# An audio tower on one core: odd DCT coefficients from 128 rotated samples, expert tiles in single PSUM banks

## The chip, the cores and the metric

The kernel runs on one core of a Trainium2 chip. The time is device microseconds of one execution; the median of three runs of the kernel before is 1459.71 us (1459.28 to 1461.03). Everything is fp32. Five engines work side by side, each through its own queue in order: TensorE (PE in the profile; its weight loads are PEld), VectorE (DVE), ScalarE (ACT), GpSimd (POOL) and SyncE (SP, which here only issues DMAs). They wait for each other through semaphores.

## The reference

64 clips of 80,000 samples are cut into 157 frames of 512 samples (the last is padded with zeros). Each frame goes through an orthonormal DCT of 512 points, and the result through one layer of attention and one of experts:

```python
h = einsum('bfh,kh->bfk', frames, DCT)          # 64 x 157 x 512
h = h + attention(layernorm(h))                  # phasor memory, causal sums, sigmoid gate, Wo
h = h + experts(layernorm(h))                    # each clip: mean over frames picks one of 16 experts
```

In the attention, keys and queries are 32 phases each; a causal sum over the frames of phase products weighs the values x Wv, a gate sigmoid(x Wg) mixes two such reads, and the result goes through Wo. In the experts, the mean of a clip's rows is routed by a softmax over 16 logits; the clip's rows are multiplied with the chosen 512 x 512 matrix and scaled by the gate.

## The kernel before

The clips go in 16 groups of four. A group has five tiles of 128 rows: the first 128 frames of each of its four clips (tiles 0 to 3), and tile 4 with the four tails of 29 frames, at 32 rows each.

**Order.** The schedule is written out by hand: instructions stand in each engine's queue in the order in which the program issues them. Group g's iteration consists of `project_and_values(g)` (projections, values; beside it routing of group g-1), `gate(g)`, `experts_and_embedding(g)` (L885: the experts of group g-1, the DCT of group g+1) and `attention(g)`. Group 0 has `first_values` and `first_gate` in place of the first three, and group 15 has no embedding, so `experts_and_embedding` runs for g = 1 to 14.

**The DCT.** `load_frame` (L85) brings a tile's samples, transposed and partly reversed by the host, as four blocks of 128 samples by 128 frames. `fold_once` (L91) makes sums `even` on VectorE (L96) and differences on GpSimd (L97, in place, blocks 0 and 1). `fold_twice` (L100) folds the sums once more on VectorE into blocks 2 and 3. `embed` (L189) then needs two matmuls with 128 columns for the even coefficients (4j and 4j+2, L201), and, for the odd ones, two matmuls with 256 columns that are summed in PSUM (L203): 256 differences against 256 odd coefficients. An fp32 matmul stands in the profile as two passes, so that L201 and L203 have four passes each for a tile. All land in one bank `h`, each coefficient in its place by a stride of four.

**The norm.** `embed_ln` (L206) takes `statistics` (L150: VectorE's bn_stats L153 and bn_aggr L155, then three small GpSimd operations L157, L158 and L160 for the reciprocal deviation `rstd` and `shift`), one more GpSimd operation for `rstd1`, and two ScalarE activations of `h`: `x`, the normed tile (L213), and `r`, the residual with the norm added (L220). `turn` (L228) transposes x with four TensorE transposes (L166) and `place` (L169) copies the result to SBUF on ScalarE (L172, L174).

**The stage of experts and embedding** issues steps in this order: E0 D0 D1 E1 T0 D2 E2 T1 D3 E3 T2 D4 E4 T3. E is `expert(g-1, m)` (L757: eight passes of 512 columns at L185, or 32 for the tails at L766, then VectorE's eviction with gate and bias L774 and the store); D is `embed`, `embed_ln` and `load_frame`; T is `turn`. After D1, D2 and D3 and T0 it also issues `fold_once` and `fold_twice` for tiles 3 and 4, `add_bias` (L755, VectorE) and `add_bv` (L348, GpSimd, 2.36 us each). `attention` begins with `read_tails(0)`, then T4, then `read_tails(2)`. The folds of tiles 0 to 2 stand in `project_and_values` and `gate`.

**PSUM.** `psum()` hands out three tiles of two banks in turn, `bank()` two single banks in turn. The embeddings, experts, products and reads use `psum()`; transposes, scores and routing use `bank()`. A tile is handed out again when its last reader is through.

Of the kernel before, what the change touches and what calls it, by code (L numbers as in the profile page):

```python
# [14 lines left out]
F32 = mybir.dt.float32  # L15
I32 = mybir.dt.int32
AF = mybir.ActivationFunctionType
ALU = mybir.AluOpType
AX = mybir.AxisListType

B, L, D = 64, 157, 512
T_IN = 80000
P = 128
# [3 lines left out]
NG = B // GB  # L27
# [3 lines left out]
NM = GB + 1  # L31
# [10 lines left out]

@with_exitstack
def audio_tower(ctx: ExitStack, tc: tile.TileContext, a, out):

# [22 lines left out]
    def load(name, shape, src=None):  # L70
        t = const.tile(shape, F32, name=name, tag=name)
        nc.sync.dma_start(out=t, in_=a[name] if src is None else src)
        return t

    def psum():

        return ps_mm.tile([P, 2, 512], F32, tag="mm", name="mm")
# [22 lines left out]
    def fold_twice(g, m):  # L100

        if g < NG:
            ft, even = S[g]["frame", m], S[g].pop(("even", m))
            nc.vector.tensor_tensor(ft[:, 2, :], even[:, 0, :], even[:, 1, :], ALU.add)
            nc.vector.tensor_tensor(ft[:, 3, :], even[:, 0, :], even[:, 1, :], ALU.subtract)


    load_frame(0, 0)
    dct_e = load("dct_e", [P, 2, P])
    dct_o = load("dct_o", [P, 2, 2 * P])  # L110
    load_frame(0, 1)
    load_frame(0, 2)
    wv = load("wv", [P, C, D])
# [36 lines left out]
    def statistics(h):  # L150

        st = small.tile([P, 6], F32, tag="st", name="st")
        nc.vector.bn_stats(st, h)  # L153
        mv = small.tile([P, 2], F32, tag="mv", name="mv")
        nc.vector.bn_aggr(mv, st)  # L155
        rstd = small.tile([P, 1], F32, tag="rstd", name="rstd")
        nc.gpsimd.tensor_scalar(rstd, mv[:, 1:2], EPS, None, ALU.add)  # L157
        nc.gpsimd.tensor_tensor(rstd, rstd, power, ALU.pow)  # L158
        shift = small.tile([P, 1], F32, tag="shift", name="shift")
        nc.gpsimd.tensor_scalar(shift, mv[:, 0:1], rstd, -1.0, ALU.mult, ALU.mult)  # L160
        return rstd, shift
# [27 lines left out]
    def embed(g, m):  # L189

        s = S[g]
        if m == 0:
            s["xT"] = p1.tile([P, C, GB, LP], F32, tag="xT", name="xT", bufs=2)
            s["xT_t"] = p1.tile([P, C, P], F32, tag="xT_t", name="xT_t")
            s["res"] = []
            s["res2"] = []
        h = psum()[:, 0, :]
        ft = s.pop(("frame", m))
        by_r = h.rearrange("p (j r) -> p r j", r=4)
        for i in range(2):  # L200
            nc.tensor.matmul(by_r[:, 2 * i, :], ft[:, 2 + i, :], dct_e[:, i, :], start=True, stop=True)  # L201
        for i in range(2):
            nc.tensor.matmul(by_r[:, 1::2, :], ft[:, i, :], dct_o[:, i, :], start=(i == 0), stop=(i == 1))  # L203
        s["h", m] = h

    def embed_ln(g, m):  # L206
        s = S[g]
        h = s.pop(("h", m))
        rstd, shift = statistics(h)
        rstd1 = small.tile([P, 1], F32, tag="rstd1", name="rstd1")  # L210
        nc.gpsimd.tensor_scalar(rstd1, rstd, 1.0, None, ALU.add)
        x = p2.tile([P, D], F32, tag="x", name="x")
        nc.scalar.activation(x, h, AF.Identity, bias=shift, scale=rstd)  # L213
        if m == GB:
            r = p1.tile([P, D], F32, tag="res_t", name="res_t", bufs=2)
        else:
            if m % 2 == 0:
                s["res2"].append(p1.tile([P, 2, D], F32, tag="res", name="res", bufs=4))
            r = s["res2"][-1][:, m % 2, :]
        nc.scalar.activation(r, h, AF.Identity, bias=shift, scale=rstd1)  # L220
        s["res"].append(r)
        s["x", m] = x
# [214 lines left out]
    fold_once(0, 1)  # L437
    fold_twice(0, 1)
    embed(0, 1)
    embed_ln(0, 0)  # L440
    warm(6)
    fold_once(0, 2)
    turn(0, 0)
    embed_ln(0, 1)
    fold_twice(0, 2)
    embed(0, 2)
    fold_once(0, 3)
    value(0, 0)
# [308 lines left out]
    def expert(g, m, between=lambda c: None):  # L757
        s = S[g]
        xT, ws = s["x2T"], s["ws"]
        ps = psum()[:, 0, :]  # L760
        if m < GB:
            by_tokens(ps, lambda c: between(c) or xT[:, c, m, :P], ws[m])
        else:
            for c in range(C):
                for i in range(GB):
                    nc.tensor.matmul(  # L766
                        ps[TL * i : TL * (i + 1), :],
                        xT[:, c, i, P:],
                        ws[i][:, c, :],
                        start=(c == 0),  # L770
                        stop=(c == C - 1),
                    )
        o = s.pop(("be", m))
        nc.vector.scalar_tensor_tensor(o, ps, s["gate"][:, m : m + 1], o, ALU.mult, ALU.add)  # L774
        if m < GB:
            nc.sync.dma_start(out=out[GB * g + m, :P, :], in_=o)
        else:

            for i in range(GB):
                for lo, hi in ((0, TL // 2), (TL // 2, LT)):  # L780
                    queue = nc.sync if g + 1 < NG else nc.scalar
                    queue.dma_start(out=out[GB * g + i, P + lo : P + hi, :], in_=o[TL * i + lo : TL * i + hi, :])
# [21 lines left out]
    def first_gate():  # L804

        by_weight = chain(weight_sums(wo, t_o), weight_sums(wv, t_v), weight_sums(wg, t_g))
        for m in range(NM):
            for n in (0, 1) if m == 0 else (m + 1,):
                if n < NM:
                    embed(1, n)  # L810
                    embed_ln(1, n)
                    load_frame(2, n)
            add_bo(0, m)
            if m < GB:
                gate_part(0, m)
                for _ in range(3):
                    next(by_weight)
                turn(1, m)
            if m < 2:
                scores(2 * m)  # L820
            elif m == 2:
                scores_of_tails()
# [62 lines left out]
    def experts_and_embedding(g):  # L885
        add_bias(g - 1, 0)
        add_bias(g - 1, 1)
        for step in ("E0", "D0", "D1", "E1", "T0", "D2", "E2", "T1", "D3", "E3", "T2", "D4", "E4", "T3"):
            what, m = step[0], int(step[1])
            if what == "E":  # L890
                expert(g - 1, m)
            elif what == "T":
                turn(g + 1, m)
            else:
                embed(g + 1, m)
                embed_ln(g + 1, m)
                load_frame(g + 2, m)
            if step == "D1":
                fold_once(g + 1, 3)
                add_bias(g - 1, 2)  # L900
                add_bias(g - 1, 3)
            elif step == "T0":
                fold_twice(g + 1, 3)
            elif step == "D2":
                add_bv(g, 0)
                fold_once(g + 1, 4)
                add_bias(g - 1, 4)
            elif step == "D3":
                fold_twice(g + 1, 4)
                add_bv(g, 1)  # L910
# [92 lines left out]
def _constants():  # L1003
    k = np.arange(D)[:, None].astype(np.float64)
    t = np.arange(D)[None, :].astype(np.float64)
    dct = np.cos(np.pi * (2.0 * t + 1.0) * k / (2.0 * D))
    scale = np.full((D, 1), np.sqrt(2.0 / D))
    scale[0, 0] = np.sqrt(1.0 / D)
    dct = (scale * dct).astype(np.float32)
    ahead, back = slice(0, P), slice(2 * P - 1, P - 1, -1)  # L1010
    odd = np.concatenate([dct[1::4], dct[3::4]])

    def trig(half, n, turn):

        rows = np.array([[-1.0, -turn, PI / 2]] * half + [[1.0, turn, 0.0]] * half)
        return np.tile(rows, (n, 1)).astype(np.float32)

    norm = 1.0 / np.sqrt(np.float64(PLANES) * (np.arange(LP) + 1))
    causal = (np.arange(LP)[:, None] <= np.arange(LP)[None, :]) * norm[None, :]
    setsel = np.tile(np.repeat(np.eye(SETS), PLANES, axis=0), (2, 1))  # L1020
    f = lambda x: np.ascontiguousarray(x, dtype=np.float32)
    return {
        "dct_e": f(np.stack([dct[0::4, ahead].T, dct[2::4, ahead].T], axis=1)),
        "dct_o": f(np.stack([odd[:, ahead].T, odd[:, back].T], axis=1)),
        "ptrig": trig(PLANES, 1, 2 * PI),
        "pos": f(np.tile(np.arange(LP), (2 * PLANES, 1))),
        "hmask": f(0.5 * causal[:P, :L]),
        "hmask_t": f(0.5 * np.kron(np.eye(GB), causal[P:, P:]).reshape(P, GB, TL)[:, :, :LT]),
        "setsel": f(setsel),
        "revexp": f(np.tile(E - np.arange(E), (P, GB, 1))),  # L1030
        "rowbase": f(np.arange(P)[:, None] + P * E),
    }
# [53 lines left out]
```

## Time and profile before

| | us |
|---|---|
| median of three runs | 1459.71 |
| profiled execution, its own time | 1460.95 |
| its span | 1459.2 |
| TensorE busy, 6866 matmul passes | 1448.2 |
| VectorE busy, 2027 instructions | 924.7 |
| GpSimd busy, 1042 | 692.1 |
| ScalarE busy, 781 | 482.3 |
| the odd half of the DCT on TensorE (L203), 320 passes, mean 382 ns | 82.8 |
| the even half (L201), 320 passes, mean 277 ns | 49.3 |

A pass of a matmul is listed from its start to its modelled end, and the next starts before that: what a pass costs TensorE is the distance between starts. A line of the timeline gives the start and the length in us, the engine, the program line, the operation with the tiles that it writes and reads, how many instructions were merged, and in brackets the idle time before it with what ended that. A line of the groups gives busy time in us and the mean of one in ns, then idle time before and what released it. The mean granted TensorE clock was 0.998 of full speed.

### The profile page before, as it was taken

The numbers are of one execution on the slowest core, as the hardware profiler recorded it, in microseconds if no ns is written. First come the engines' busy times: TensorE is split into PE (matmuls) and PEld (weight loads), VectorE is DVE, ScalarE is ACT, GpSimd is POOL, SyncE is SP. The second block draws the span as 40 slices with busy tenths as digits, with TensorE's granted clock in tenths as the row PEclk, the third lists the DMA queues.
The fourth block names the chain that finished last, engine by engine and source line by source line (L and its number), as shares of the span: only waits on it lengthen the run. The fifth ranks groups of instructions, "written<-read, shape, count | busy, mean of one in ns | idle before, by whom it ended". The sixth has DMA issues, their size and how long they took to land.

```text
span 1459.2 us, 19271 instructions
## 1 busy us (share of the span) xinstructions
PE 1448.2 (99%) x6866; PEld 1008.9 (69%) x6866; DVE 924.7 (63%) x2027; ACT 482.3 (33%) x781; POOL 692.1 (47%) x1042
## 2 busy tenths in 40 slices
PE   9999999999999999999999999999999999999998
PEld 6776676767767677676766767667676776766763
DVE  5676665656666576665765757666566665666573
ACT  4532143422433323343232432324332243422410
POOL 4454545445354453554435553455534545445422
PEclk9999999999999999999999999999999999999999
DMA  5105142050320404214041230413205142040305
GB/s 195 37 1 188 36 152 72 3 200 22 152 72 31 178 15 156 68 65 152 7 173 50 108 113 4 180 43 135 89 1 188 36 152 72 1 173 15 152 7 216
DMA packets 42862, 135.36 MB, mean 93 GB/s; under 512 B 7872, under 2 KB 8400, under 8 KB 34192
## 3 DMA queue, kind: packets, MB, share of 16 engines
q0 software_dynamic: 15616, 88.09, 15.8%
q1 hardware_dynamic: 26920, 45.81, 9.9%
q8 instruction: 55, 0.90, 0.2%
q10 hardware_dynamic: 232, 0.24, 0.1%
q14 instruction: 39, 0.32, 0.1%
HBM read 113.53 MB, written 20.58 MB: 92 GB/s over the span
## 4 chain that ended last, share of the span: by engine, by line
PE 95%; DMA 2%; DVE 1%; POOL 1%; issue 1%; ACT 0%; SPq 0%; POOLq 0%; DVEq 0%
PE mm L283 26%; PE mm L185 22%; PE mm L542 15%; PE mm L583 9%; PE tr L166 5%; PE mm L203 4%; PE mm L766 4%; PE mm L488 2%; PE mm L201 2%; PE mm L596 2%; PE tr L666 1%; PE tr L559 1%; PE mm L524 1%; DMA be_last<-in_be,expi 1%; DMA frame<-in_frames 1%
## 5 line engine op out<-in xcount | busy, mean ns | idle before, releaser
L185 PE MATMUL mm<-we,x2T 128*128 128x512 f32 x496 | 223.2, 593 | 0.0
L157 POOL TENSOR_SCALAR rstd<-mv 128x1 f32<-128x1 f32 x160 | 47.3, 296 | 309.1 <-DVE mv L155 302.5
L185 PEld LDWEIGHTS mm<-we,x2T 128*128 128x128 f32 x496 | 92.7, 190 | 95.9 <-issue 89.6
L583 PE MATMUL mm<-att,v 128*128 128x314 f32 x512 | 139.8, 431 | 2.4 <-DVE of_tails L574 2.4
L286 DVE TENSOR_TENSOR gT<-mm,gT 128x628 f32<-128x628 f32 x105 | 85.5, 814 | 86.0 <-PE mm L542 84.7
L774 DVE SCALAR_TENSOR_TENSOR be<-mm,gate,be 128x512 f32<-128x512 f32 x75 | 56.3, 751 | 126.3 <-PE mm L185 87.1
L213 ACT ACTIVATE x<-mm,shift,rstd 128x512 f32<-128x512 f32 x80 | 62.2, 777 | 224.0 <-POOL shift L160 224.0
L583 PEld LDWEIGHTS mm<-att,v 128*128 128x128 f32 x512 | 98.2, 192 | 39.3 <-issue 4.0
L286 DVE TENSOR_TENSOR v<-mm,v 128x512 f32<-128x512 f32 x105 | 72.4, 689 | 75.8 <-PE tr L166 50.5
L552 ACT ACTIVATE gT<-gT,hbg 128x314 f32<-128x314 f32 x120 | 60.4, 551 | 166.1 <-DVE gT L286 166.1
L158 POOL TENSOR_TENSOR rstd<-rstd,power 128x1 f32<-128x1 f32 x160 | 108.3, 677 | 13.3
L166 PEld LDWEIGHTS tr<-ident,x 128*128 128x128 f32 x576 | 69.4, 141 | 51.4 <-issue 36.3
L611 POOL TENSOR_TENSOR res<-res,u 128x512 f32<-128x512 f32 x48 | 60.2, 1268 | 73.4 <-DVE u L286 73.4
L166 PE MATMUL tr<-ident,x 128*128 128x128 f32 x576 | 88.2, 276 | 1.2 <-DVE x2T L174 0.5
L707 POOL DMA_INDIRECT we<-in_we,rows x62 | 61.6, 994 | 57.0 <-PE mm L185 40.6
L283 PE MATMUL mm<-t_o,sum 128*128 128x256 f32 x384 | 88.1, 379 | 0.0
L153 DVE BATCH_NORM_STATS2 st<-mm 128x6 f32<-128x512 f32 x80 | 55.9, 699 | 50.7 <-PE mm L203 50.7
L604 POOL TENSOR_TENSOR tT_t<-gT,of_tails 128x116 f32<-128x116 f32 x64 | 30.5, 498 | 119.4 <-DVE gT L574 117.3
L283 PE MATMUL mm<-t_v,sum 128*128 128x256 f32 x360 | 86.7, 384 | 0.0
L283 PEld LDWEIGHTS mm<-t_o,sum 128*128 128x128 f32 x384 | 73.1, 190 | 16.7 <-issue 7.7
L286 DVE TENSOR_TENSOR res<-mm,res 128x512 f32<-128x512 f32 x96 | 64.5, 685 | 29.6 <-PE mm L283 18.9
L203 PE MATMUL mm<-dct_o,frame 128*128 128x256 f32 x320 | 82.8, 382 | 0.0
(189 smaller groups left out, 2988.7 us busy)
## 6 DMA issues: line engine op xcount, KB each, us to landing
frame<-in_frames SPq DMA_DIRECT2D x80, 256.0 KB
out<-be SPq DMA_DIRECT2D x60, 256.0 KB
out<-be SPq DMA_DIRECT2D x60, 32.0 KB
out<-be SPq DMA_DIRECT2D x60, 26.0 KB
be<-in_be,expi POOLq DMA_INDIRECT x75, 8.8
wv<-in_wv SPq DMA_DIRECT2D x1, 1024.0 KB
wg<-in_wg SPq DMA_DIRECT2D x1, 1024.0 KB
wo<-in_wo SPq DMA_DIRECT2D x1, 1024.0 KB
```

What stands on the lines that cost most here:

```text
L158: nc.gpsimd.tensor_tensor(rstd, rstd, power, ALU.pow)
L166: nc.tensor.transpose(tr[:, c * P : (c + 1) * P], x[:, c * P : (c + 1) * P], ident)
L185: nc.tensor.matmul(ps, lhs(c), w[:, c, :], start=(c == 0), stop=(c == C - 1))
L203: nc.tensor.matmul(by_r[:, 1::2, :], ft[:, i, :], dct_o[:, i, :], start=(i == 0), stop=(i == 1))
L213: nc.scalar.activation(x, h, AF.Identity, bias=shift, scale=rstd)
L283: nc.tensor.matmul(ps[:, b, :], lhs[:, c, b, :P], w[:, c, :], start=(c == 0), stop=(c == 1))
L286: add = lambda to, x, y: nc.vector.tensor_tensor(to, x, y, ALU.add)
L542: nc.tensor.matmul(ps[:, o, : 2 * L], w[:, c, o * P : (o + 1) * P], rhs[:, c], start=(c == 0), stop=(c == 1))
L552: nc.scalar.activation(to, to, AF.Tanh, bias=hbg[:, c : c + 1], scale=0.5)
L583: nc.tensor.matmul(ps[:, c, : 2 * L], s["v", i][:, cols], att[:, i], start=True, stop=True)
L611: more = lambda to, x: nc.gpsimd.tensor_tensor(to, to, x, ALU.add)
L707: nc.gpsimd.indirect_dma_start(out=w, out_offset=None, in_=a["we"], in_offset=bass.IndirectOffsetOnAxis(ap=s["rows"][:, b : b + 1], axis=0),)
```

## The change

The odd coefficients are computed in another way. With angle a_t = pi (2t+1)/1024 for t = 0 to 127, each pair of differences (p, q) of a sample is rotated by a_t; the coefficients 4j+1 are then the sum, and 4j-1 the difference, of a cosine sum and a sine sum over 128 samples at the angle 4 j a_t. VectorE does the rotation as two lifting steps at the end of `fold_twice` (p + tan(a) q, then q - sin(a) cos(a) p, with [128, 1] scalars `lift`), and the remaining scales are folded into the constant `dct_o`. The two matmuls have 129 columns each (j = 0 to 128) and are not summed: they land apart in the second bank of the tile. A new function `embed_statistics` copies the sine sums to SBUF on ScalarE (VectorE then has one input in PSUM and one in SBUF), adds and subtracts on VectorE into the places of `h`, and takes the statistics.

The order changes too: in the stage of experts and embedding, the statistics of tiles 0 and 1 come after D1, one after the other, and then the two `embed_ln`; in `first_gate` the first two tiles are treated alike, and at the start of the program the statistics of both first tiles come before the first `embed_ln`. The experts of groups 0 to 13 use `bank()` in place of `psum()`. Matmuls, sums and stores of all other parts stay.

```diff
@@ fold_twice
             nc.vector.tensor_tensor(ft[:, 3, :], even[:, 0, :], even[:, 1, :], ALU.subtract)
+            for n in range(2):
+                to, by = ft[:, n, :], ft[:, 1 - n, :]
+                nc.vector.scalar_tensor_tensor(to, by, lift[:, n : n + 1], to, ALU.mult, ALU.add)
@@
     dct_e = load("dct_e", [P, 2, P])
-    dct_o = load("dct_o", [P, 2, 2 * P])
+    lift = load("lift", [P, 2])
+    dct_o = load("dct_o", [P, 2, P + 1])
@@ embed
-        h = psum()[:, 0, :]
+        h = psum()
+        h, odd = h[:, 0, :], h[:, 1, :].rearrange("p (n j) -> p n j", n=2)
...
         for i in range(2):
-            nc.tensor.matmul(by_r[:, 1::2, :], ft[:, i, :], dct_o[:, i, :], start=(i == 0), stop=(i == 1))
-        s["h", m] = h
+            nc.tensor.matmul(odd[:, i, : P + 1], ft[:, i, :], dct_o[:, i, :], start=True, stop=True)
+        s["h", m] = h, odd
+
+    def embed_statistics(g, m):
+        s = S[g]
+        h, odd = s.pop(("h", m))
+        by_r = h.rearrange("p (j r) -> p r j", r=4)
+        sines = p2.tile([P, P + 1], F32, tag="sines", name="sines")
+        nc.scalar.copy(sines, odd[:, 1, : P + 1])
+        nc.vector.tensor_tensor(by_r[:, 1, :], odd[:, 0, :P], sines[:, :P], ALU.add)
+        nc.vector.tensor_tensor(by_r[:, 3, :], odd[:, 0, 1 : P + 1], sines[:, 1 : P + 1], ALU.subtract)
+        s["st", m] = h, *statistics(h)
@@ embed_ln
-        h = s.pop(("h", m))
-        rstd, shift = statistics(h)
+        if ("st", m) not in s:
+            embed_statistics(g, m)
+        h, rstd, shift = s.pop(("st", m))
@@ start of the program
     embed(0, 1)
+    embed_statistics(0, 0)
+    embed_statistics(0, 1)
     embed_ln(0, 0)
     warm(6)
     fold_once(0, 2)
     turn(0, 0)
+    fold_twice(0, 2)
     embed_ln(0, 1)
-    fold_twice(0, 2)
@@ expert
-        ps = psum()[:, 0, :]
+        ps = bank() if g + 2 < NG else psum()[:, 0, :]
@@ first_gate
-            for n in (0, 1) if m == 0 else (m + 1,):
-                if n < NM:
-                    embed(1, n)
-                    embed_ln(1, n)
-                    load_frame(2, n)
+            new = [n for n in ((0, 1) if m == 0 else (m + 1,)) if n < NM]
+            for step in (embed, embed_statistics, embed_ln):
+                for n in new:
+                    step(1, n)
+            for n in new:
+                load_frame(2, n)
@@ experts_and_embedding, step D
                 embed(g + 1, m)
-                embed_ln(g + 1, m)
-                load_frame(g + 2, m)
+                if m > 0:
+                    new = (0, 1) if m == 1 else (m,)
+                    for n in new:
+                        embed_statistics(g + 1, n)
+                    for n in new:
+                        embed_ln(g + 1, n)
+                        load_frame(g + 2, n)
@@ constants
-        "dct_o": f(np.stack([odd[:, ahead].T, odd[:, back].T], axis=1)),
+        "dct_o": f(np.stack([cosines, sines], axis=1)),
+        "lift": f(np.concatenate([np.tan(angle), -np.sin(angle) * np.cos(angle)], axis=1)),
```

More of the change, by code (lines that the diff above doesn't have):

```diff
@@ L1009, in _constants @@
     dct = (scale * dct).astype(np.float32)
-    ahead, back = slice(0, P), slice(2 * P - 1, P - 1, -1)
-    odd = np.concatenate([dct[1::4], dct[3::4]])
+    ahead = slice(0, P)
+    angle = np.pi * (2.0 * np.arange(P)[:, None] + 1.0) / (2.0 * D)
+    j = np.arange(P + 1)[None, :]
+    cosines = np.sqrt(2.0 / D) * np.cos(angle) * np.where(j < P, np.cos(4 * j * angle), 0.0)
+    sines = np.sqrt(2.0 / D) / np.cos(angle) * np.sin(4 * j * angle)
     def trig(half, n, turn):
```

## The prediction

> **What bounds the kernel now.** I read the busy shares first, then the chain of waits, then the timeline of one middle round of `experts_and_embedding` (g = 6: experts of group 5, embedding of group 7), and the groups by shape for prices.
>
> ```profile
> PE 1448.2 (99%) x6866; PEld 1008.9 (69%) x6866; DVE 924.7 (63%) x2027; ACT 482.3 (33%) x781; POOL 692.1 (47%) x1042
> ...
> PE 95%; DMA 2%; DVE 1%; POOL 1%; issue 1%; ACT 0%; SPq 0%; POOLq 0%; DVEq 0%
> ```
>
> TensorE is busy nearly all the span and carries 95% of the chain: any matmul time removed counts in full, and so does any hole made in TensorE's work. The timeline shows the round (start, length, engine, line):
>
> ```profile
> 578.03 3.60 PE L185 MATMUL mm<-we,x2T 128*128 128x512 f32 x8
> 581.46 0.61 PE L201 MATMUL mm<-dct_e,frame 128*128 128x128 f32 x4
> 581.91 1.03 PE L203 MATMUL mm<-dct_o,frame 128*128 128x256 f32 x4
> 582.77 0.61 PE L201 MATMUL mm<-dct_e,frame 128*128 128x128 f32 x4
> ...
> 585.02 0.18 DVE L155 BATCH_NORM_AGGREGATE mv<-st 128x2 f32<-128x6 f32 x1
> 585.12 0.39 DVE L96 TENSOR_TENSOR even<-frame 128x256 f32<-128x256 f32 x1
> ...
> 585.42 1.41 DVE L755 SCALAR_TENSOR_TENSOR be<-be,gate,res 128x512 f32<-128x512 f32 x2
> 585.66 0.57 POOL L157 TENSOR_SCALAR rstd<-mv 128x1 f32<-128x1 f32 x1
> ...
> 586.32 0.94 POOL L158 TENSOR_TENSOR rstd<-rstd,power 128x1 f32<-128x1 f32 x1
> 587.36 0.26 POOL L160 TENSOR_SCALAR shift<-mv,rstd 128x1 f32<-128x1 f32 x1
> ...
> 587.66 0.78 ACT L213 ACTIVATE x<-mm,shift,rstd 128x512 f32<-128x512 f32 x1 [0.95 <-POOL shift L160]
> ...
> 588.34 0.77 ACT L220 ACTIVATE res<-mm,shift,rstd 128x512 f32<-128x512 f32 x1
> ...
> 589.00 0.58 ACT L172 COPY xT<-tr 128x512 f32<-128x512 f32 x1
> ...
> 602.11 0.78 ACT L213 ACTIVATE x<-mm,shift,rstd 128x512 f32<-128x512 f32 x1 [3.00 <-POOL shift L160]
> ...
> 604.58 0.60 PE L166 MATMUL tr<-ident,x 128*128 128x128 f32 x4
> ```
>
> Starts give the pace, since lengths overlap: four 128-column passes take 0.45 us (581.46 to 581.91), four 256-column ones 0.86. Call E, D, T the expert, embedding and transposes of a tile (E 3.43, D 1.31, T 0.44); a step E, T, D is 5.18. With E0 at 0 (578.03), the last transpose T4 starts at 26.55, and its x was ready at 24.86. The prices:
>
> ```profile
> L573 DVE TENSOR_TENSOR gT<-mm,gT 128x314 f32<-128x314 f32 x128 | 61.7, 482 | 7.1 <-PE mm L583 4.8
> ...
> L172 ACT COPY xT<-tr 128x512 f32<-128x512 f32 x64 | 37.4, 584 | 6.7 <-PE tr L166 6.6
> ...
> L104 DVE TENSOR_TENSOR frame<-even 128x128 f32<-128x128 f32 x80 | 22.4, 280 | 7.8 <-POOL frame L97 6.9
> ...
> L573 DVE TENSOR_TENSOR of_tails<-mm,gT 128x232 f32<-128x232 f32 x32 | 12.8, 399 | 13.6 <-PE mm L596 13.6
> ```
>
> [...] the place copy of T0, whose transposes were through by 588.2, begins at 589.00, behind two activations. The forecast rests on this. [...] GpSimd's power (L158) takes 0.57 beside VectorE work from PSUM and 0.94 beside L755. [...]
>
> **The change, part by part.**
>
> *TensorE.* The odd half goes from four passes of 256 columns to four of 129: 0.86 to 0.45 us. Saved 0.41 a tile, 2.05 a group of five, 33 us over 80 tiles. This is certain. D becomes 0.90, the step 4.77.
>
> *VectorE, lifts.* Two dependent scalar_tensor_tensor of 128 columns in fold_twice. L755 takes 746 ns at 512; [...] some 0.73 a tile with the gap between. Those of tiles 0 to 2 lie where VectorE has room: the one in the gate stage ends 0.7 later, and the next gT product is late by 0.7 but still ends before the following one arrives (1.3 us of idle there). Price nothing; without that cover 0.7 each. Tiles 3 and 4 stand in the embedding stage: lift 3 ends at about 12, before its engine has the next sums to make, and lift 4 is in the sum below.
>
> *VectorE, adds.* No row writes PSUM from VectorE. From the two L573 rows (83 ns for 82 columns) a 128-column sum with a PSUM input is 0.29. The second waits for the first (dependent pairs in the trace run 0.03 apart): 0.64 for both until bn_stats. [...] I take 0.64: nothing in the trace punishes stride, since L201 writes PSUM with that stride at the pace of its columns.
>
> *ScalarE, sines.* [...] It stands in ScalarE's queue behind x, r and place of the earlier tile, and VectorE's adds, statistics, and then the next expert's eviction wait behind it.
>
> *Banks.* E now shares two banks with T: E(k+1) waits until E(k) is evicted. After E(k) TensorE has only T and D, 1.34 us, to cover an eviction of 0.95 (0.20 delay and 0.75); any queue before it on VectorE over 0.4 us shows as a hole.
>
> *SP.* Frame 0's load is issued with frame 1's, a round ahead of its use: nothing. The smaller dct_o and the tiny lift load come before the first embedding, which waited for frame folding: nothing.
>
> **The sum for one round** (starts, us after E0; delays from the trace: 0.20 after a matmul, 0.09 to GpSimd, 0.03 to 0.05 otherwise).
> D0 ends 4.33, D1 5.23. Sines0 4.53, adds0 4.83, bn_stats 5.47, aggregate 6.21; adds1 6.31, bn_stats 6.95, aggregate 7.69. Tile 0: GpSimd 6.48 to 7.73, x0 until 8.55, T0 at 8.66 just in time. GpSimd's statistics of tile 1 start 7.96 beside L96 and L755 as before: 1.96 (585.66 to 587.62), until 9.92. rstd1 of tile 0 now stands behind them: r0 10.13, then x1 10.79, r1 11.47, place 12.13, sines2 12.61. (Before, place T0 was at 10.97, and no VectorE work waited for it.)
> From here a loop closes over four engines, once a tile: sines to adds 0.30, adds 0.64, bn_stats 0.74, aggregate to GpSimd 0.27, GpSimd 1.67 (590.47 to 592.14), 0.04, then on ScalarE x 0.68, r 0.66, place 0.48, next sines: 5.48. TensorE's step is 4.77, so the loop sets the pace. Sines3 18.09, sines4 23.57, x4 26.81 to 27.59, T4 27.65 against 26.55.
> TensorE meets it as holes: E2 0.2 (E1's eviction stands behind two L755); E3 1.2 (E2's eviction 15.4 to 16.2, behind aggregate 2, L96 and L755); E4 0.8 (E3's behind lifts 4, ending 21.0); T4 1.05 for x4. 3.25, less 2.05 saved and 0.1 of an old gap: +1.1 a round.
> Attention after it, and the next group's first stages, run at TensorE's pace as before, so nothing gives this back: 14 rounds, +15.4.
>
> Group 0: its embeddings of group 1 stand between gate parts (4.3 us each), five tiles save 2.05, but gate part 0 waits for keep_value(4), now behind lift 3 (+0.7), and gate part 1 for r1, later by the adds, by rstd1's place and by two lifts: 1.5 to 2.5 late with the saving already taken, and something comes back after. The first five embeddings: x0 about 1.2 later, four cheaper tiles after it, and a frame transfer until 27.4 behind that. Together +2 (between -2 and +5).
>
> The profiled execution took 1460.95 (span 1459.2): 1460.95 + 15.4 + 2 = 1478.3. The median of the runs is 1.24 lower: 1477.1.
>
> **Rivals.**
> *A, the saving stays.* The loop at 4.77 or less a step, 0.7 cheaper than summed, is where this decides: ScalarE's sines would find the queue empty, evictions come in the 1.34 us cover. For it: VectorE would be busy under 80% of the stage, ScalarE half. Against: a share says nothing of order, and the place behind r and place is fixed. Then 14 times 2.05 is kept, group 0 even: 1459.7 - 28.7 = 1431. Not slower.
> *B, a draw.* Adds pair at 0.52 (-0.12 five times), GpSimd at 1.38 as beside L104 today (twice -0.29): the round falls by 1.2 to -0.1 and the time to 1458, between 1452 and 1462 with group 0's bounds.
> *C, strided PSUM writes are dear.* Pair at 1.16: five in the chain, +2.6 a round, 3.7 in all: 1459.7 + 52 + 5 = 1517. For it: no row shows such a write; against: the reads and matmuls above.
>
> **How the numbers follow.** Forecast 0.68, its own range 1463 to 1501 (pair 0.56 and GpSimd 1.5: +0.4 a round, 5 and -2; pair 0.86 and GpSimd 1.96: +2.8 a round, 39 and 2). A 0.10, B 0.14, C 0.08. The range 1455 to 1500 leaves out A, C and an edge of B. Runs tell 0.2%, 2.9 us. Faster: A and half of B less a little, 0.16; same: 0.08; slower: the rest, 0.76.
>
> **What would show it.** Right: D at 0.90 us; holes of about a microsecond before E3, E4 and T4 in every round from group 1, the releaser VectorE's eviction for the experts and ScalarE's x for T4; sines to sines near 5.5. TensorE's busy time down by some 30 us with the span up. Wrong: a gapless step of 4.77 (A); adds far from 0.29 (C); sines starting at once after D, the loop not closed; holes in the gate stage or the attention, which I count at nothing.

## The result and the profile after

| | before | after |
|---|---|---|
| median of the runs, us (lowest to highest) | 1460.85 (1459.28 to 1462.65) | 1481.61 (1480.20 to 1484.69) |
| profiled execution, us (span) | 1460.95 (1459.2) | 1481.61 (1479.5) |
| first read of attention in group 0 (L583, after L603), us | 68.23 | 80.92 |
| a middle round, from E0 to the next E0, us | 89.59 | 90.27 |
| E0 to T4 in that round, us | 26.55 | 27.16 |

The kernel is slower by 1.5%: ratio 1.0150, 95% interval 1.0134 to 1.0165. Ratios, here and below, are of the executions within 1.5% of the fastest of the same kernel, which leaves out 9 of the 22 of e11_bv_in_gate and no others. The span grew by 20.3 us, in two places: 12.7 before the first read of group 0, and 14 rounds of 0.68, together 9.5. Some 1.7 came back in the last group, so that these three add up to 20.5. First the busy shares and the chain of waits of after:

```profile
PE 1435.4 (97%) x6866; PEld 988.8 (67%) x6866; DVE 1019.3 (69%) x2347; ACT 494.6 (33%) x861; POOL 685.5 (46%) x1042
...
PE 72%; DVE 9%; ACT 8%; POOL 6%; issue 3%; DMA 1%; SPq 0%; POOLq 0%; DVEq 0%
```

TensorE's share of the chain fell from 95% to 72%, and VectorE, ScalarE and GpSimd hold 23% in its place: a chain over several engines now sets part of the end. The groups by shape of after (count, then busy us and mean ns, then idle time before them and its releaser) hold the prices:

```profile
L110 DVE SCALAR_TENSOR_TENSOR frame<-frame,lift 128x128 f32<-128x128 f32 x160 | 55.7, 348 | 2.8
...
L210 PE MATMUL mm<-dct_o,frame 128*128 128x129 f32 x320 | 52.1, 285 | 0.0
...
L220 DVE TENSOR_TENSOR mm<-mm,sines 128x128 f32<-128x128 f32 x80 | 23.9, 299 | 2.7
L219 DVE TENSOR_TENSOR mm<-mm,sines 128x128 f32<-128x128 f32 x80 | 23.5, 294 | 85.6 <-ACT sines L218 85.6
L218 ACT COPY sines<-mm 128x129 f32<-128x129 f32 x80 | 22.3, 280 | 50.3 <-PE mm L210 50.3
```

The odd matmuls fell from 82.8 us to 52.1. Nothing that was added is dear by itself; what stands out is the 85.6 us that VectorE waits for ScalarE's copies of sine sums of 280 ns each. The timeline of one middle round of after (E0 at 594.11) shows the loop once, for tile 2, and its start for tile 3:

```profile
603.66 0.61 PE L210 MATMUL mm<-dct_o,frame 128*128 128x129 f32 x4
...
605.31 0.78 ACT L238 ACTIVATE res<-mm,shift,rstd 128x512 f32<-128x512 f32 x1
...
605.97 0.59 ACT L178 COPY xT<-tr 128x512 f32<-128x512 f32 x1
...
606.43 0.30 ACT L218 COPY sines<-mm 128x129 f32<-128x129 f32 x1
...
606.76 0.30 DVE L219 TENSOR_TENSOR mm<-mm,sines 128x128 f32<-128x128 f32 x1 [0.79 <-ACT sines L218]
...
607.43 0.70 DVE L159 BATCH_NORM_STATS2 st<-mm 128x6 f32<-128x512 f32 x1
...
608.43 0.29 POOL L163 TENSOR_SCALAR rstd<-mv 128x1 f32<-128x1 f32 x1 [3.64 <-DVE mv L161]
...
609.23 0.74 DVE L794 SCALAR_TENSOR_TENSOR be<-tr,gate,be 128x512 f32<-128x512 f32 x1
...
610.03 3.70 PE L191 MATMUL tr<-we,x2T 128*128 128x512 f32 x8 [0.67 <-DVE be L794]
...
610.15 0.78 ACT L231 ACTIVATE x<-mm,shift,rstd 128x512 f32<-128x512 f32 x1 [3.42 <-POOL shift L166]
...
611.96 0.29 ACT L218 COPY sines<-mm 128x129 f32<-128x129 f32 x1
...
615.60 3.64 PE L786 MATMUL tr<-we,x2T 128*32 128x512 f32 x32 [0.17 <-DVE be L794]
...
621.27 0.66 PE L172 MATMUL tr<-ident,x 128*128 128x128 f32 x4 [0.66 <-ACT x L231]
```

D2 was through at about 604.11 (four passes after 603.66), but its sines were copied at 606.43, behind r and the place copy of earlier tiles. VectorE waited for them, so the statistics, and behind these the eviction of E2 (609.23), came late, and TensorE stood for 0.67 us before E3 (610.03). From sines to sines it is 5.53 us, and 5.21 to the next (617.17). Before E4 (615.60) TensorE stood 0.17 and before T4 (621.27), which waited for x4, 0.66.

Now group 0, TensorE alone on the timeline of after:

```profile
12.24 0.66 PE L172 MATMUL tr<-ident,x 128*128 128x128 f32 x4 [1.82 <-ACT x L231]
14.14 0.71 PE L208 MATMUL mm<-dct_e,frame 128*128 128x128 f32 x4 [1.25 <-DVE frame L106]
...
15.58 4.99 PE L191 MATMUL mm<-wv,xT 128*128 128x512 f32 x8
...
27.66 0.66 PE L172 MATMUL tr<-ident,x 128*128 128x128 f32 x4 [0.95 <-ACT x L231]
```

T0 starts 1.27 us later than before (10.97), D2 another 1.4 later (14.14 against 11.47), and the value product then takes 4.83 from start to start where it took 3.44. D2 waited for a fold (L106): the new order at the start of the program puts the statistics of tile 1 ahead of that fold's difference in GpSimd's queue, so that the difference began at 13.04 and not at 10.25. The stretches of 8 us (length, busy us and instructions of the five engines, granted clock, DMA share, GB/s) show what the clock did:

```profile
16.00:24.00 8.00, 8.00 (x26) 4.09 (x25) 6.75 (x24) 4.33 (x9) 4.27 (x10) 0.85 0.94 314
24.00:32.00 8.00, 6.56 (x28) 3.61 (x26) 5.14 (x22) 2.58 (x5) 2.08 (x6) 1.00 0.51 146
32.00:40.00 8.00, 6.70 (x17) 3.03 (x16) 4.71 (x16) 3.81 (x5) 3.62 (x13) 0.79 0.00 0
```

After holes, TensorE's clock was halved for two stretches of 3.4 us (14.96 to 18.38 and 35.44 to 38.85), 1.7 us lost in each; in before the clock's record, which begins at 7.20 us, has none in this group (its first embedding, at 5.35, ran at half pace: 0.86 us for four passes of 128 columns). Of the 12.7 us these are 3.4; the rest are waits. Two of them are ScalarE's queue again, which here also holds the load of a table. The sines of tile 3, whose matmuls were through at 21.74, stood behind the load, and those of tile 4, through at 26.56, behind x, r and place copies:

```profile
21.84 1.28 ACT L412 ACT_TABLE_LOAD   x1
23.14 0.52 ACT L412 ACTIVATE pf<-folded,ptrig 16x160 f32<-16x160 f32 x1
23.56 0.24 ACT L218 COPY sines<-mm 128x129 f32<-128x129 f32 x1
23.84 0.30 DVE L219 TENSOR_TENSOR mm<-mm,sines 128x128 f32<-128x128 f32 x1 [0.20 <-ACT sines L218]
...
29.12 0.30 ACT L218 COPY sines<-mm 128x129 f32<-128x129 f32 x1
...
29.45 0.30 DVE L219 TENSOR_TENSOR mm<-mm,sines 128x128 f32<-128x128 f32 x1 [2.19 <-ACT sines L218]
```

The table load cost VectorE only 0.20 us, since its own folds and lifts lasted until 23.63; the queue cost it 2.19 for tile 4. The transposes of tile 3 began at 27.66 in place of 23.15, those of tile 4 at 33.33 in place of 27.02. When TensorE begins the first embedding of group 1 (46.46 against 38.51), 8.0 of the 12.7 us are lost; the other 4.7 come in `first_gate`, where TensorE waits 1.74 us for the tail values and 0.78, 1.29 and 1.52 for x and r.

### The profile page after: what moved, and what is told of

Read it like the earlier page. It is cut to its first block, busy times and chain, and to the rows that moved or that the text cites. A ratio compares the mean times of both kernels' runs of the same rounds, so it can differ in the third digit from the quotient of the medians.

```text
span 1479.5 us, 19617 instructions
## 1 busy us (share of the span) xinstructions
PE 1435.4 (97%) x6866; PEld 988.8 (67%) x6866; DVE 1019.3 (69%) x2347; ACT 494.6 (33%) x861; POOL 685.5 (46%) x1042
## 4 chain that ended last, share of the span: by engine, by line
PE 72%; DVE 9%; ACT 8%; POOL 6%; issue 3%; DMA 1%; SPq 0%; POOLq 0%; DVEq 0%
PE mm L301 26%; PE mm L562 15%; PE mm L603 9%; PE mm L191 8%; DVE st L159 4%; PE tr L172 3%; PE tr L191 3%; POOL rstd L164 3%; ACT x L231 3%; ACT res L238 3%; PE mm L508 2%; DVE mm L220 2%; ACT xT L178 2%; DVE mm L219 2%; POOL rstd L163 1%
## 5 line engine op out<-in xcount | busy, mean ns | idle before, releaser
L191 PE MATMUL tr<-we,x2T 128*128 128x512 f32 x448 | 204.3, 599 | 10.2 <-DVE be L794 9.3
L163 POOL TENSOR_SCALAR rstd<-mv 128x1 f32<-128x1 f32 x160 | 44.0, 275 | 357.7 <-DVE mv L161 351.0
L191 PEld LDWEIGHTS tr<-we,x2T 128*128 128x128 f32 x448 | 81.6, 190 | 98.1 <-issue 80.4
L603 PE MATMUL mm<-att,v 128*128 128x314 f32 x512 | 138.2, 427 | 2.4 <-DVE of_tails L594 2.4
L603 PEld LDWEIGHTS mm<-att,v 128*128 128x128 f32 x512 | 97.1, 190 | 38.7 <-issue 2.9
L572 ACT ACTIVATE gT<-gT,hbg 128x314 f32<-128x314 f32 x120 | 60.4, 551 | 166.0 <-DVE gT L304 154.5
L219 DVE TENSOR_TENSOR mm<-mm,sines 128x128 f32<-128x128 f32 x80 | 23.5, 294 | 85.6 <-ACT sines L218 85.6
L764 POOL DMA_INDIRECT be<-in_be,expi x75 | 71.2, 950 | 22.9 <-issue 18.6
L244 POOL TENSOR_TENSOR res<-res,bo 128x512 f32<-128x512 f32 x64 | 80.2, 1281 | 0.0
```

The source lines that it names most:

```text
L191: nc.tensor.matmul(ps, lhs(c), w[:, c, :], start=(c == 0), stop=(c == C - 1))
L244: nc.gpsimd.tensor_tensor(r, r, bo, ALU.add)
L572: nc.scalar.activation(to, to, AF.Tanh, bias=hbg[:, c : c + 1], scale=0.5)
L603: nc.tensor.matmul(ps[:, c, : 2 * L], s["v", i][:, cols], att[:, i], start=True, stop=True)
L764: nc.gpsimd.indirect_dma_start(out=be, out_offset=None, in_=a["be"], in_offset=bass.IndirectOffsetOnAxis(ap=s["expi"][:, m : m + 1], axis=0),)
```

## The experiments

The theories are these. *Queue*: the copy's place in ScalarE's queue closes the loop of the prediction. *Banks*: experts in single banks wait for their evictions. *Work*: VectorE simply has too much to do. For group 0: waits and the clock. All kernels start from after; e8 is built on e1, e10 on e8 and e9, e11 on e10 and e12 on e11. The table has what every one measured (us); "first read" and "round" are the marks of the table above.

| run | median | ratio to before, 95% interval | first read | round |
|---|---|---|---|---|
| e1_sines_vector | 1459.56 | 0.9992 (0.9983 to 1.0000) | 79.08 | 88.77 |
| e2_sums_unbound | 1484.05 | 1.0155 (1.0138 to 1.0172) | 82.36 | 90.25 |
| e3_experts_in_pairs | 1488.11 | 1.0192 (1.0175 to 1.0209) | 79.31 | 90.65 |
| e4_no_lifts | 1478.02 | 1.0122 (1.0105 to 1.0138) | 76.75 | 90.25 |
| e5_two_copies | 1502.37 | 1.0280 (1.0259 to 1.0301) | 82.03 | 91.48 |
| e6_sums_free | 1441.59 | 0.9864 (0.9844 to 0.9884) | 75.27 | 87.78 |
| e7_warm_start | 1481.33 | 1.0136 (1.0119 to 1.0153) | 79.07 | 90.27 |
| e9_old_first_groups | 1472.88 | 1.0083 (1.0066 to 1.0100) | 68.51 | 90.24 |
| e8_evict_first | 1478.77 | 1.0119 (1.0104 to 1.0133) | 77.19 | 90.17 |
| e10_both | 1469.57 | 1.0055 (1.0042 to 1.0068) | 68.62 | 90.17 |
| e11_bv_in_gate | 1475.64 | 1.0063 (1.0046 to 1.0080) | 69.12 | 88.26 to 92.37 |
| e12_bv_on_vector | 1442.94 | 0.9879 (0.9863 to 0.9895) | 68.85 | 88.26 |

**Sines copied by VectorE.**

```diff
-        nc.scalar.copy(sines, odd[:, 1, : P + 1])
+        nc.vector.tensor_copy(sines, odd[:, 1, : P + 1])
```

> The changed kernel, with the copy of the sine sums made by VectorE in place of ScalarE; 0.28 us more of VectorE's time a tile, no ScalarE in the way of the sums. A middle round (distance of the first expert of one group to that of the next) is 90.27 us in the changed kernel, 89.59 before. Queue theory (the sines' place in ScalarE's queue closes a loop of 5.2 to 5.5 us a tile): the loop is cut, the round falls to about 89.3 and the time by about 13 us, to 1468. Work theory (VectorE has too much to do in the stage): the round rises to 90.6 or more, the time to 1487. Bank theory (experts and transposes sharing two banks makes the holes): no change, 90.3.

The round fell by 1.5 us, more than the queue theory had (to 89.3) and below that of before, although VectorE got more to do (1036.5 us busy against 1019.3). The timeline of this kernel's round (E0 at 584.75) has the loop opened:

```profile
596.89 0.28 DVE L218 COPY sines<-mm 128x129 f32<-128x129 f32 x1
596.98 0.59 ACT L178 COPY xT<-tr 128x512 f32<-128x512 f32 x1
...
599.76 0.61 PE L210 MATMUL mm<-dct_o,frame 128*128 128x129 f32 x4
...
600.41 0.29 DVE L218 COPY sines<-mm 128x129 f32<-128x129 f32 x1
600.48 3.70 PE L191 MATMUL tr<-we,x2T 128*128 128x512 f32 x8
```

The sines of tile 3 come 3.52 us after those of tile 2, and 0.2 after their matmuls; the place copy no longer stands ahead of them. This speaks for the queue and against the work. The time is still no better than before, since group 0 keeps 10.9 us of its loss.

**Sums that read a constant, the copy kept.**

```diff
         nc.scalar.copy(sines, odd[:, 1, : P + 1])
+        sines = hold
```

> The changed kernel, where the sums and differences read a constant tile of the same shape in place of the copied sine sums (that leaves the sine half of the odd coefficients out of the result); ScalarE still makes every copy, VectorE has the same operations, only the wait of VectorE for ScalarE's copy is gone. Queue theory: the round falls from 90.27 to about 88.7 us, the last transpose comes some 25.6 us after the first expert in place of 27.16, the time falls by about 20 us to 1460. Work theory and bank theory: 90.2, within 3 us of the changed kernel.

It failed as a test: the wait was not gone. The waits of this kernel (total us, times, longest) show it at the same size as in after (85.6 us, 62 times):

```profile
DVE mm L222 <- ACT sines L220: 86.2, 62, 3.2
```

The sums no longer read what ScalarE writes, but they write into the tile that ScalarE's copy reads, in another bank of it; that order is kept too, as the next run bears out.

**The copy freed as well.**

```diff
-        nc.scalar.copy(sines, odd[:, 1, : P + 1])
+        nc.scalar.copy(sines, hold)
+        sines = hold
```

> As the run in which the sums read a constant, but ScalarE's copy now also reads a constant and not the embedding's PSUM tile, so that VectorE's writes into that tile have no reader on ScalarE to wait for (the sine half is left out of the result). Queue theory: now the loop is cut, the round is 88.3 to 88.8 us. Work and bank theory: 90.2 us, as VectorE, ScalarE and the banks have the same to do.

With the work of the engines left as in after and the tie between ScalarE and VectorE cut, the round is 87.78: the tie costs 2.49 us a round. (The copy, 308 ns here, no longer waits for TensorE's matmuls either; what that alone is worth was not separated.) The saving of TensorE alone would give 89.59 - 2.05 = 87.54, so nearly all of it is there. This is the strongest result for the queue.

**A second copy, as a dose.**

```diff
         nc.scalar.copy(sines, odd[:, 1, : P + 1])
+        nc.scalar.copy(sines, odd[:, 1, : P + 1])
```

> The changed kernel with the copy of the sine sums made twice by ScalarE, one after the other. Queue theory: each of the four copies that stand in the chain (tiles 0, 2, 3 and 4) adds 0.2 to 0.27 us, the last transpose comes 0.8 to 1.1 later and the round is 91.1 to 91.4 us in place of 90.27; the time rises by 11 to 16 us. Bank and work theory: ScalarE is busy a third of the time, nothing changes, 90.3 us.

Five copies of 0.27 us more in each round, 1.34 us on an engine that is a third busy, and the round grew by 1.21: nearly all of them are paid for. That is a little more than expected (91.48, not 91.1 to 91.4), and the time rose by 20.8 us and not by 11 to 16: 2.8 us of this lie in the last group, where a wait of 1.49 us came that after does not have (see e11).

**Experts in pairs of banks again.**

```diff
-        ps = bank() if g + 2 < NG else psum()[:, 0, :]
+        ps = psum()[:, 0, :]
```

> The changed kernel with every expert's tile from the three tiles of two banks again, as before the change. Bank theory: the holes before the experts go and the round falls to 88.5 or less, the time by 25 us. Queue theory: the holes only move, since an embedding's tile is held until its residual is written by ScalarE; the round is 90.3 to 90.7 us, the time between the same and 6 us more.

Slower by 0.38 a round than after. The timeline of its round says what waits:

```profile
605.07 0.71 PE L208 MATMUL mm<-dct_e,frame 128*128 128x128 f32 x4 [1.42 <-ACT res L238]
...
611.92 3.70 PE L191 MATMUL mm<-we,x2T 128*128 128x512 f32 x8 [0.92 <-ACT res L238]
```

The tile of an embedding is held until r has read it, which is late in the same loop; experts that share these buffers wait for it. The single banks are a gain, not the cause.

**No lifts.** The two lifting steps of `fold_twice` are taken out.

> The changed kernel without the two lifting steps of fold_twice (the rotation is left out of the result): 0.73 us less of VectorE's time a tile, 3.65 a group. Work theory: the round falls by at least the 1.46 us of the two tiles folded in the stage, to 88.8 or less. Queue theory: the lifts are beside the loop, only the hole before the last expert may shrink; the round stays within 90.0 to 90.3 us. Group 0 (first read of the attention at 80.92 us in the changed kernel, 68.23 before) gains 1 to 3 us, since lifts stand ahead of its first embeddings and its first gate part.

The round stays (90.25): in the rounds 0.73 us a tile on VectorE is hidden, against the work theory. The first read comes 4.17 earlier, more than the expected 1 to 3. There is no half-clock stretch in group 0 in this run, which alone is 3.4 of the 4.17; so the lifts were not free there, but their own share was not separated from the clock's.

**A warmer start.**

```diff
     embed_ln(0, 0)
-    warm(6)
+    warm(12)
     fold_once(0, 2)
     turn(0, 0)
+    warm(6)
```

Four and two more such matmuls stand around the transposes of tile 3, four ahead of those of tile 4.

> The changed kernel with more matmuls of the identity in the places of group 0 where TensorE waits (before the first and the fourth and fifth transposes, and before the third embedding). The changed kernel's record has two stretches of 3.4 us at half clock in group 0, the kernel before none there. Clock theory (the waits of group 0 cost twice, in themselves and by 1.7 us of clock for each stretch): no such stretch is left, the first read of the attention comes at 77.5 to 79 us in place of 80.92, the time falls by 2 to 3.4 us; the rounds stay at 90.27. Wait theory (only the waits count): no change, or the added matmuls' own time, up to 1 us more.

The clock stayed at 1.00 in all of the first 72 us, yet the first read came only 1.85 earlier, at 79.07, just outside what the clock theory had. Of the 3.4 us at stake about half came back; the waits remain, and how much the added matmuls took themselves was not separated. The time did not change: in the profiled execution the last group, from its predecessor's E0 to the end, took 165.1 us in place of 163.2, with a wait of 1.49 for the gate's gT that after does not have (see e11).

**The first two groups as before.** Groups 0 and 1 are embedded in the old way and order, all later groups in the new one.

```diff
-            for n in range(2):
+            for n in range(2 if g > 1 else 0):
@@ embed
+            if g > 1:
+                nc.tensor.matmul(odd[:, i, : P + 1], ft[:, i, :], dct_o[:, i, :], start=True, stop=True)
+            else:
+                nc.tensor.matmul(by_r[:, 1::2, :], ft[:, i, :], dct_w[:, i, :], start=(i == 0), stop=(i == 1))
@@ embed_statistics
+        if g < 2:
+            s["st", m] = h, *statistics(h)
+            return
```

> The changed kernel with the embeddings of groups 0 and 1 made in the old way: old order, 256-column odd matmuls summed in PSUM with their own constant, no lifts, no copies, no sums; groups 2 to 15 as changed. If all of the loss of group 0 comes from the new embeddings and their order there, the first read comes at 68.2 to 68.5 us (80.92 changed, 68.23 before), the rounds stay at 90.27 us and the time is 1469 to 1471 us. If the smaller transfers or the bank change carry part of it, the first read stays above 70 us.

The first read is at 68.51, 0.28 from before, and the round is untouched: the 12.4 us belong to the embeddings of the first two groups and their order. The time fell by 8.7 only, the profiled span by 10.0, since the last group gave some back: from its predecessor's E0 to the end this kernel needs 166.0 us and after 163.2, with a wait of 1.40 us for the gate's gT that after does not have, and 1.69 in place of 0.60 before the last expert.

**VectorE's order changed** (on top of e1): both `fold_once` stand after D1, the bias additions of tiles 2 to 4 stand behind the evictions of E1, E2 and E3, and the last `fold_twice` stands after E2 in place of D3.

```diff
             if step == "D1":
                 fold_once(g + 1, 3)
+                fold_once(g + 1, 4)
+            elif step == "E1":
                 add_bias(g - 1, 2)
-                add_bias(g - 1, 3)
...
+            elif step == "E2":
+                add_bias(g - 1, 3)
+                fold_twice(g + 1, 4)
...
+            elif step == "E3":
                 add_bias(g - 1, 4)
```

> The run with VectorE's copy of the sine sums, and VectorE's queue put in another order in the stage: the eviction of expert 1 ahead of both bias additions, that of expert 2 and of expert 3 ahead of the next bias addition and the last fold, both folds' differences on GpSimd ahead of the value bias. If what is left of the saving there (round 88.77 us, 87.5 would be 89.59 less the 2.05 of TensorE) is lost to evictions that stand behind other work, the round falls to 87.5 to 87.8 us and the time to about 1444 us. If it is lost to VectorE's or GpSimd's sheer work, the round stays at 88.5 or more.

**Both together**, this order and the old first groups.

> The former together with the old embeddings for groups 0 and 1. First read at 68.2 to 68.5 us, rounds at 87.5 to 87.8 us: 14 rounds each 1.8 to 2.1 us shorter than before, 1432 to 1436 us. If group 0 and the rounds do not add up (the first rounds starting with other waits), more than 1440 us.

Both missed: 90.17 a round, all the gain of e1 lost. The timeline of e10_both shows what neither expectation held:

```profile
597.61 2.71 DVE L110 SCALAR_TENSOR_TENSOR frame<-frame,lift 128x128 f32<-128x128 f32 x2
597.74 2.43 POOL L373 TENSOR_TENSOR v<-v,bv 128x1024 f32<-128x1024 f32 x1
```

Two lifts that take 0.73 elsewhere took 2.71: the new order put them beside GpSimd's addition of the value bias. In after the same addition (610.25 to 612.60) stood beside an idle VectorE and, from 612.27, its sums that read PSUM. Lift and addition ended within 0.15 us of each other, at 600.32 and 600.17; what the two share was not shown. E4 then stood 1.18 us.

**The additions moved into the gate's stage** (on top of e10):

```diff
         fold_once(g + 1, 2)
+        if g + 1 < NG:
+            add_bv(g, 0)
+            add_bv(g, 1)
@@ experts_and_embedding
             elif step == "D2":
-                add_bv(g, 0)
...
             elif step == "D3":
-                add_bv(g, 1)
```

> The kernel of e10_both with one move: GpSimd's two additions of the value bias to the tail values (L373, 2.4 us each) are issued in the gate's stage, after the fold's difference, and no longer inside the experts' stage after D2 and D3. Path theory ([...] the two lifts took 2.71 us in place of 0.73 in e10_both): the lifts of tile 3 and 4 fall back to 0.7 to 0.9 us a pair, the hole of 1.18 us before E4 shrinks to 0.2 or less, the wait of T4 (0.43) goes, the middle round falls from 90.17 to 87.5 to 88.2 us and the time from 1469.6 to 1433 to 1443 us. Order theory (VectorE's new queue order itself is at fault, the long lift only a bystander): the hole before E4 stays near 1.2 us and the round at 89.8 to 90.3, the time at 1465 to 1471. If the additions now stand beside two-input work of VectorE in the gate's stage, something of it comes back there: up to 1 us a round.

In the experts' stage of an undisturbed round it came as the path theory has it, with the addition no longer beside the lifts: these took 0.73, the wait of T4 went, and seven of the thirteen rounds of the profiled execution (1464.35 us) took 88.3 us or less. But three took 90.65 to 90.67, with a wait of 2.1 us in the gate's stage, and three 92.35 to 92.37, where a half-clock stretch followed that wait. The timeline of this kernel in one such round:

```profile
1013.86 5.49 DVE L595 TENSOR_TENSOR att_t<-att_t,share_t 128x116 f32<-128x116 f32 x1
1013.88 0.73 POOL L99 TENSOR_TENSOR frame<-frame 128x256 f32<-128x256 f32 x1
1014.56 4.64 POOL L373 TENSOR_TENSOR v<-v,bv 128x1024 f32<-128x1024 f32 x2
...
1020.13 2.12 PE L567 MATMUL mm<-sum,wg 128*128 128x314 f32 x7 [2.13 <-DVE gT L311]
```

An addition of 116 columns, 0.28 us in an undisturbed round (569.46, ahead of GpSimd's 570.19), started 0.02 us before GpSimd's first instruction here and lay through all three, 5.49 us; the gate's sums behind it came late, and TensorE waited 2.13 us for room. In all six disturbed rounds this addition started between 0.49 us after and 0.06 before GpSimd's first instruction, in the undisturbed ones at least 0.68 before it. Who is first is thus decided by a fraction of a microsecond, which fits the spread of the executions, from 1456 to 1492 us, where before stayed within 3 us on the same chip; only one of them was profiled.

The same race explains the waits in the last group. There GpSimd's two additions stand in the gate's stage in every kernel, before included. In before and after the small addition came 0.86 and 0.68 us ahead and took 0.28; in e5, e7, e8 and e9 it took 4.80 to 5.43 us, and TensorE waited 1.40 to 1.49. In e7:

```profile
1395.96 5.43 DVE L594 TENSOR_TENSOR att_t<-att_t,share_t 128x116 f32<-128x116 f32 x1
1396.58 4.67 POOL L366 TENSOR_TENSOR v<-v,bv 128x1024 f32<-128x1024 f32 x2
```

**The additions given to VectorE** (on top of e11), where it was idle:

```diff
-        nc.gpsimd.tensor_tensor(v, v, bv.unsqueeze(1).to_broadcast([P, 2, D]), ALU.add)
+        engine.tensor_tensor(v, v, bv.unsqueeze(1).to_broadcast([P, 2, D]), ALU.add)
@@ gate
                 scores_of_tails()
+                if g + 1 < NG:
+                    add_bv(g, 0)
@@ experts_and_embedding
         add_bias(g - 1, 1)
+        add_bv(g, 1)
```

> The kernel of e11_bv_in_gate with the two value-bias additions (L373) given to VectorE, where it stood idle in an undisturbed round of that run: one after the attention scores of the tails (idle 569.75 to 571.83), one between the two expert biases and the first eviction of the experts' stage (580.71 to 582.00); GpSimd keeps them in the last group alone. Path theory (the rounds of 90.65 and 92.36 us in e11_bv_in_gate, against 88.26, came from VectorE's small addition at L595 being held 5.5 us by GpSimd's 4.6 us of additions, and the 4.1 us ones from a half-clock stretch after that wait): with no GpSimd addition of 1024 columns beside VectorE no round is disturbed, all thirteen read 88.0 to 88.5 us, the time is 1464.4 - 19.5 = 1445 us, 1440 to 1449, the same from run to run within 4 us; the additions cost 1.1 to 1.2 us each. Rival (VectorE's queue is now so full that its own order sets the end): the gate's products or the first sines come late by up to a microsecond, all rounds alike at 88.8 to 89.6 us, and the time is 1452 to 1464.

All thirteen rounds read 88.24 to 88.26, and the time is 1442.94 (1442.66 to 1444.44): 1.2% faster than before, 2.6% than after. The timeline of this kernel's VectorE:

```profile
562.86 0.28 DVE L595 TENSOR_TENSOR att_t<-att_t,share_t 128x116 f32<-128x116 f32 x1
563.05 1.22 DVE L373 TENSOR_TENSOR v<-v,bv 128x1024 f32<-128x1024 f32 x1
...
574.23 1.22 DVE L373 TENSOR_TENSOR v<-v,bv 128x1024 f32<-128x1024 f32 x1
```

GpSimd needed 2.4 us for what VectorE does in 1.22. The kernel is the changed one from group 2 on, with VectorE's sines, the new order and these additions; no run tells what each of them is worth without the others. Of the remaining 0.72 us over 87.54, 0.43 is the hole before E3, where `fold_twice` of tile 3 waits 0.97 us for GpSimd's difference and its first instruction then takes 0.80 us in place of 0.28, beside GpSimd's next difference.

## Why the prediction was right, and where it was not

The direction and the mechanism of the rounds held, and the time is 4.5 us from the forecast of 1477.1. That it is so near is in part luck, since two terms were off in opposite directions. Measured against the profiled executions, 1478.3 was predicted and 1481.61 came: rounds 5.9 less than the sum, group 0 10.7 more, the last group 1.7 less.

- *TensorE's saving*: right, 0.45 us for the four passes (597.98 to 598.43). Its busy time fell by 12.8 and not 30, since each hole lays the end of a pass open (a product of 3.43 us from start to start counts 3.60 or 3.70) and the half clock stretches others; in e12, with few holes and two groups embedded in the old way, it is 24.7.
- *Adds, sines, lifts*: right, 294 and 299 ns, 280, 348. From the first add to bn_stats it is 0.67 (606.76 to 607.43), predicted 0.64. The sum's 0.73 for a pair of lifts and 0.30 from sines to adds, and the 0.52 and 1.16 of rivals B and C for the pair of adds, were my guesses: no row of before shows them. Rival C, dear strided writes, is out.
- *The loop*: right in its members and its place, as e1, e5 and e6 show, a little short in size. The first turn took 5.53, the second 5.21, predicted 5.48 for both: GpSimd took 1.69 in the one (608.43 to 610.12), its power 0.94 beside VectorE's bias addition L775, and 1.39 in the other (613.95 to 615.34), its power 0.57 beside the lifts; this had been rival B's term. The start was earlier too, sines 2 at 12.32 and not 12.61, since the statistics of tile 1 took 1.69 and not 1.96. So T4 came at 27.16 and not 27.65.
- *Holes*: they are in the places forecast, and smaller. From start to start, which is how the sum counts them, E2 cost 0.3 (predicted 0.2), E3 0.9 (1.2), D4 and E4 together 0.7 (0.8) and T4 0.8 (1.05): 2.8 and not 3.25. The idle times in the brackets are less, since the end of the pass before a hole counts as busy. The round grew by 0.68, not 1.1: 9.5 us in place of 15.4.
- *Rival A* lost in after. Of the 2.05 us a round that it would have kept, e1 has 0.82, e12 1.33 and e6, which leaves the sine half out of its result, 1.81: its deciding point, sines that do not stand in a queue, is right.
- *Group 0*: the term that was mis-sized. I put it at +2, between -2 and +5; it measured +12.7. x0's delay was right (1.27, predicted 1.2). But the sum then let cheaper tiles make up for it, while the trace has 8.0 us lost by the first embedding of group 1: D2 waits for a fold that stands in GpSimd's queue, the clock is halved twice (3.4), and the sines of tile 4 stand in ScalarE's queue. `first_gate` lost another 4.7, where the sum had 1.5 to 2.5. The queue argument that I had made for the rounds was not carried to the start, where all queues hold other things. e9 shows that the 12.4 us go with the embeddings of these two groups and their order; how they split between lifts, sines and order was not settled. e4 moves the first read by 4.2, of which 3.4 go with the clock; e6 moves it by 5.7 with two half-clock stretches, as many as in after, so that the tie between ScalarE and VectorE accounts for a good part here too.
- *The last group*: not in the sum. Before had one half-clock stretch there (1.7 us at about 1390), after has none, though both have the same wait of 2.42 us (it ends at 1389.59 and at 1411.80). What tells them apart was not shown, so I do not put the 1.7 us down to the change.

## What to carry to other kernels

A short instruction on an engine that is a third busy can set the pace if its queue closes a loop (the copies of 280 ns here held up a round by 2.49 us, by e6): sum the loop over all engines and ask which member may stand in another queue. When an order is changed, look at which neighbours it creates on GpSimd and VectorE. Here two lifts of 0.73 us took 2.71 beside a GpSimd addition of 2.4 us (e10), and an addition of 0.28 us took 5.49 beside three GpSimd instructions (e11); with an order in which they raced, the time of e11 went from 1456 to 1492 us from run to run, and with the additions given to VectorE that of e12 stayed within 1.8 us. Sum the first group apart from the rounds, with its own queues.

## What the runs showed of the hardware

- In e11 a VectorE addition of 116 columns that by the profile started 0.02 us before GpSimd's first instruction lay through three GpSimd instructions in a row, 5.49 us in place of the 0.28 us of an undisturbed round. In before and after that small addition took 0.87 to 0.94 us when it started up to 0.61 us ahead of GpSimd's difference of 0.73 to 0.84 us, and 0.28 to 0.31 us when it was 0.68 or more ahead of GpSimd's next difference or addition; in e7, 0.62 us ahead of the two additions, it took 5.43.
- Stretches at half clock were 3.41 us long in before and after (the end of the program apart). In the record of after the clock's changes stand whole multiples of 3.41 us apart: 10.24 from the start of the record to the first, then 3.41, 17.07 and 3.41. The idle time of TensorE alone does not tell which wait is followed by half clock. In e11_bv_in_gate, six waits of 2.12 to 2.15 us in the same place were followed by it three times (those that end at 307.55, 1110.81 and 1293.82) and not the other three. In the last group before's wait of 2.42 us was followed by it (clock 0.50 from 1389.60 to 1393.00), after's of the same length was not (1.00 from 1405 to 1425). In group 0 of after 1.30 us idle in the 3.41 us ahead (32.03 to 35.44) were followed by half clock too. What decides was not shown, and no threshold can be read from these waits.
- VectorE's sums of 128 columns, written with a stride of four into PSUM, took 294 and 299 ns in after; its sums of 128 columns written to SBUF took 280 and 287 ns in before.
